# Layer statistics and a normalization moved to ScalarE in a fused feed-forward, attention, feed-forward kernel

## The chip, the cores and the metric

One Trainium2 chip, of which the kernel uses one core. The metric is the device time of one launch in microseconds. An execution varies from launch to launch, so the time is a median of three runs.

## The reference

The input `x` has 16 sequences of 256 tokens with 256 features, all in float32. Three layers follow each other, each with a residual:

```python
x = x + 0.5 * ffn(layernorm(x), w1, b1, w2, b2)
x = x + attention(layernorm(x), Wq, Wk, Wv, Wo)
x = x + 0.5 * ffn(layernorm(x), w1, b1, w2, b2)
```

`layernorm` subtracts the mean over the features and divides by `sqrt(var + 1e-5)`. `ffn` is `gelu(x @ w1q.T + b1) @ w2q.T + b2` with 1024 hidden features, and `w1q`, `w2q` are the weights rounded to three values (-1, 0, 1 after scaling by the mean of their magnitudes). `attention` has 16 heads of 16 features, rotary positions, a causal mask and a softmax over the keys.

So every token needs a mean and a variance three times: before the first feed-forward (statistics 0), before attention (statistics 1) and before the second feed-forward (statistics 2).

## The kernel before

All of `x` stays in SBUF as eight blocks of 512 tokens, `xs[0]` to `xs[7]`. A block is four tiles of 128 tokens, and a sequence is two tiles, so a block holds two sequences. All instructions of an engine run in the order in which the Python code issues them: the helper `InOrder` (line 197, which is why nearly every row of the profile says L197) pins that order. There is no planner. The order is written by hand.

The program has three stretches. The first is the feed-forward over eight blocks (`ffn(0, ...)`), in steps of one 128-feature slice of the hidden layer, eight steps a block. The second is attention, and the third is the second feed-forward. Each overlaps the next a little.

**Attention runs in turns.** The loop at line 827 runs turn `b` from 1 to 14, and each turn has eight slots `p` (line 828); `slot` (line 736) issues all the work of a slot. In turn `b` each slot takes two heads of sequence `b` through the scores with queries as rows (PSUM tiles `m`, whose row maxima VectorE takes) and two heads of sequence `b - 1` through the scores with keys as rows (PSUM tile `w`, to which VectorE adds the mask and of which ScalarE takes the exponential into `pT`). Beside that the slots carry, a piece each, the projections of sequence `b + 1`, its rotation (`rotate`), its split into a rounded part and a rest (`part`), the DMAs that place it head by head (`place`), the weighted sums of sequences `b - 1` and `b - 2` (`attend`, `turn_sums`, `divide`, `turn_out`), and the output projection of `b - 2`.

The order of a slot on each engine, as far as it matters here:

- TensorE: the score matmuls first. There are two `m` buffers, and a slot fills both, so the scores of the next slot wait until VectorE has taken the maxima out of them. Then the slot's projections and sums.
- VectorE: four maxima (`masked`, L641) with their accumulator reads, then the mask addition (`w<-w,mask_k`, L657), then what else the slot has: in slots 1 and 5 the transpose `avs`, in slots 2 and 6 `inv`, in slots 4 and 7 the transpose `oT`, and statistics.
- ScalarE: copies out of PSUM as projections finish, the exponential (L660), and in slots 1 and 5 the copy `parts<-maxes` that starts the splitting of the maxima (`part_max`, L542). Slots 3 and 6 have the rounding copy of `part`.
- GpSimd: in slot 0 the normalization of a coming sequence (`ready_x(b + 2)`, L758), then in slots 1 and 2 the three small operations of `part_max`, the rotation's `cosT`, `sinT` and the sum, and the product `o` (`divide`, L689). In slot 3 comes `split` (`part`), and in slots 4 to 6 the same chain once more for the other eight heads, ending with the second `part`.

**Where statistics come from.** `stats` (L208) is a pair on VectorE, `bn_stats` and `bn_aggr`, for a tile of 128 tokens. `finish_stats` (L213) turns the variances of several tiles into `rstd` with two small GpSimd operations, `var` and `rstd`. For attention, `after_first` (L444) puts a block's four pairs and its `finish_stats` into the list `later`; the first feed-forward takes one off each step. Ten entries, those of blocks 6 and 7, are left when the turns begin, and the turns take them off in slots 1, 3, 5 and 7 (L792): turn 1 has four pairs, turn 2 a `finish_stats` in slot 1 and pairs in 3, 5 and 7, turn 3 a pair in slot 1 and the last `finish_stats` in slot 3. For the second feed-forward, `last_stats` (L725) takes the eight tiles of the first two blocks in slot 3 of turns 6 to 13, a pair a turn, with a `finish_stats` every second turn (turns 7, 9, 11, 13).

`normalize` (L223) is one `tensor_scalar` (subtract the mean, multiply by `rstd`) on the engine that it is given; `ready_x` (L467) calls it for the two tiles of a sequence, and inside the turns that engine is GpSimd.

Of the kernel before, what the change touches and what calls it, by code (L numbers as in the profile page):

```python
# [8 lines left out]
FP = mybir.dt.float32  # L9
FR = mybir.dt.float32r  # L10
BF = mybir.dt.bfloat16
AF = mybir.ActivationFunctionType
ALU = mybir.AluOpType
# [3 lines left out]
P = 128  # L17
D = 256
# [12 lines left out]
def kernel(  # L31
# [15 lines left out]
    NB = NT // S  # L47
    NTILE = NT // P
# [5 lines left out]
    state = ctx.enter_context(tc.tile_pool(name="state", bufs=1))  # L54
    small = ctx.enter_context(tc.tile_pool(name="small", bufs=4))
# [54 lines left out]
    for at in range(0, P, HD):  # L110
        r, n = at // 32, at // HD % 2
# [53 lines left out]
    power = const.tile([P, BT], FP, name="power")  # L165
# [19 lines left out]

    mv = [state.tile([P, NTILE, 2], FP, name=f"mv_{i}") for i in range(3)]
    rstd = [state.tile([P, NTILE], FP, name=f"rstd_{i}") for i in range(3)]

    class InOrder:

# [10 lines left out]
    tensor, vector, scalar, gpsimd, sync = (  # L201
        InOrder(engine) for engine in (nc.tensor, nc.vector, nc.scalar, nc.gpsimd, nc.sync)
    )

    def tokens(n):
        return xs[n // BT][:, n % BT, :]

    def stats(ln, n):  # L208
        st = small.tile([P, 6], FP, name="st")
        vector.bn_stats(st, tokens(n))  # L210
        vector.bn_aggr(mv[ln][:, n, :], st)

    def finish_stats(ln, first, n):  # L213

        var = small.tile([P, BT], FP, name="var")
        gpsimd.tensor_scalar(
            var[:, 0:n], mv[ln][:, first : first + n, 1], LN_EPS, 1.0, ALU.add, ALU.mult
        )
        gpsimd.tensor_tensor(
            rstd[ln][:, first : first + n], var[:, 0:n], power[:, 0:n], ALU.pow  # L220
        )

    def normalize(ln, n, to, engine=None):  # L223
        (engine or vector).tensor_scalar(
            to,
            tokens(n),
            mv[ln][:, n, 0:1],
            rstd[ln][:, n : n + 1],
            ALU.subtract,
            ALU.mult,  # L230
        )
# [210 lines left out]
    later = []  # L442
# [8 lines left out]
    xn_a, xnT, qkT, o, oT, y_a = {}, {}, {}, {}, {}, {}  # L451
# [15 lines left out]
    def ready_x(b, engine=gpsimd):  # L467
        xn_a[b] = pp.tile([P, 2, D], FP, name="xn_a", bufs=1)
        for c in range(2):
            normalize(1, 2 * b + c, xn_a[b][:, c, :], engine)  # L470

    def turn_x(b):

        tp = ps_mm.tile([P, KC, S], FP, name="mm")
        for k in range(KC):
            for c in range(2):
                tensor.transpose(
                    tp[:, k, c * P : (c + 1) * P], xn_a[b][:, c, k * P : (k + 1) * P], ident
                )
        xnT[b] = pp.tile([P, KC, S], FP, name="xnT_a", bufs=3)  # L480
        scalar.copy(xnT[b], tp)
# [31 lines left out]
    def part(b, j):  # L513
        high = split[j][:, 0:2, :]
        scalar.copy(high, qk[j])
        gpsimd.tensor_sub(split[j][:, 3:1:-1, :], qk[j], high.bitcast(FP))
# [147 lines left out]
    def attend(b, half):  # L664

        av = ps_mm.tile([P, 2, S], FP, name="mm")
        for n in range(2):
            g = 2 * half + n
            for c in range(2):
                for r in range(4):  # L670
                    tensor.matmul(
                        av[32 * r : 32 * r + 32, n, c * P : S],
                        vals[b % 2][:, c, 4 * g + r, :],
                        pT[b, 2 * g + r // 2][:, r % 2, c * S : S + c * P],
                        start=(c == 0),
                        stop=(c == 1),
                    )
        sums[b, half] = av
# [40 lines left out]
    def add_out(b):  # L719
        y, tiles = y_a.pop(b)  # L720
        at = 2 * b % BT + tiles[0]
        xt = xs[2 * b // BT][:, at : at + len(tiles), :]
        vector.tensor_add(xt, y, xt)

    def last_stats(b, c):  # L725
        stats(2, 2 * b + c)
        if c == 1:
            finish_stats(2, 2 * b, 2)

# [4 lines left out]
    def slot(b, p, more=lambda: None):  # L736
        bw, bm = (n if 0 <= n < NB else None for n in (b - 1, b))
        up, now, past, last = (n if 0 <= n < NB else None for n in (b + 1, b, b - 1, b - 2))
        first = 0 if b == NB - 1 else 1
        if p == 0 and 0 <= b - 3 < NB:  # L740
            add_out(b - 3)
        if p == 6 and last is not None and b < NB - 1:
            add_out(last)
        weigh = scores(bw, p, bm, p ^ 1)
        if p == first and last is not None:
            attend(last, 1)
        if p == 5:
            if b + 2 < NB:
                turn_x(b + 2)
            if last is not None and b < NB - 1:  # L750
                project_out(last, range(1))
        for n, j, at in ((now, 0, 5), (past, 1, 1)):
            if n is not None and p == at:
                part_max(n, j)
        if p == 3 and past is not None:
            turn_max(past, 1)
        if p == 0 and b >= 1 and b + 2 < NB:
            ready_x(b + 2)  # L758
        for n, at in ((past, p + 8), (now, p)):
            slots = VALUES.get(n, (2, 6))  # L760
            if n is not None and at in slots:
                project_v(n, slots.index(at))
        if p in (0, 3) and up is not None:
            project_qk(up, p // 2, 0 if b == 0 and p == 0 else 1)
        if p == 2 and up is not None:
            project_qk(up, 1, 0, 1)
        if p in (1, 2, 4, 5) and up is not None:
            rotate(up, p // 4, *((0,) if p in (1, 4) else (1, 2)))
        if p == 4 and past is not None:
            attend(past, 0)  # L770
        if up is not None and p == 4:
            place(up, 0)
        if now is not None and p == 0:
            place(now, 1)
        if p == 6 and now is not None:
            turn_max(now, 0)
        if p == 7:
            if last is not None and b < NB - 1:
                project_out(last, range(1, 2))
            if b + 2 < NB:  # L780
                project_qk(b + 2, 0, 0, 1)
        more()
        weigh()
        if up is not None and p in (3, 6):
            part(up, p // 3 - 1)
        for n, half, at in ((last, 1, p - first), (past, 0, p - 4)):
            if n is not None and at in (0, 1, 3):
                (turn_sums, divide, None, turn_out)[at](n, half)
        if p == 3 and b - 6 in range(8):
            last_stats(*divmod(b - 6, 2))  # L790

        if b >= 1 and p % 2 == 1 and later:  # L792
            later.pop(0)()


# [29 lines left out]
    for p in range(FFN_STEPS - HEAD, 8):  # L825
        slot(0, p)
# [116 lines left out]
```

## Time and profile before

| | |
|---|---|
| median of 3 runs | 581.95 us (579.21 to 584.72) |
| the profiled execution | 581.4 us, of which the span of the profile is 579.6 us |
| TensorE | busy 560.1 us (97%) |
| VectorE | busy 473.2 us (82%) |
| GpSimd | busy 382.5 us (66%) |
| ScalarE | busy 361.8 us (62%) |
| the turns (1 to 14) | from about 164 us to 414 us of the span |

In the profile PE is TensorE, DVE VectorE, ACT ScalarE, POOL GpSimd and SP the queue that issues most DMAs. The shares of busy time are averages over three stretches with different limits: VectorE is busy 16 of every 20 us at 80 to 100 us and 19.7 of 20 us at 300 to 320 us. A row of the timeline gives the start, the duration, the engine, the operation, the tile written and the tiles read, and in brackets how long the engine had been idle and who ended that.

### The profile page before, as it was taken

How to read it: one execution, taken by the hardware profiler on the slowest of the kernel's cores; microseconds unless marked ns; L12 is line 12 of the kernel's file. 1: busy time of each engine (PE TensorE's matmuls, PEld its weight loads, DVE VectorE, ACT ScalarE, POOL GpSimd, SP SyncE). 2: the span in 40 equal slices, each digit the busy share in tenths (PEclk: the TensorE clock that was granted, in tenths of full speed). 3: DMA queues.
4: the chain of work that ended last, by engine and by line, in shares of the span. 5: the costliest groups of instructions: out<-in, count | busy, mean ns of one | idle time of the engine just before them, and what ended most of it. 6: DMA issues, size and time to landing. Idle time of an engine off the chain costs nothing.

```text
span 579.6 us, 15188 instructions
## 1 busy us (share of the span) xinstructions
PE 560.1 (97%) x5654; PEld 454.8 (78%) x5654; DVE 473.2 (82%) x1691; ACT 361.8 (62%) x637; POOL 382.5 (66%) x427
## 2 busy tenths in 40 slices
PE   3999999999999999999999999999989999999996
PEld 3788999888777677777777777777767889888886
DVE  6887778789688999999999999999986566666653
ACT  4666777675555665656666666565566666666664
POOL 4636656668478878888888988888832455445542
PEclk9999999999988999999999999999999999999999
DMA  8700000020533464544645535445500011111111
GB/s 284 236 1 2 1 1 1 28 64 26 120 93 92 112 148 98 123 106 116 147 109 123 124 94 142 121 119 129 126 6 1 1 37 36 38 37 37 37 37 36
DMA packets 35641, 46.23 MB, mean 80 GB/s; under 512 B 4464, under 2 KB 27120, under 8 KB 35568
## 3 DMA queue, kind: packets, MB, share of 16 engines
q1 hardware_dynamic: 35008, 44.35, 29.5%
q8 instruction: 44, 0.72, 0.5%
q10 hardware_dynamic: 560, 0.92, 0.4%
q14 instruction: 29, 0.24, 0.1%
HBM read 7.51 MB, written 4.19 MB: 20 GB/s over the span
## 4 chain that ended last, share of the span: by engine, by line
PE 80%; DVE 9%; issue 3%; ACT 3%; DMA 2%; POOL 2%; SPq 0%; DVEq 0%; POOLq 0%; ACTq 0%
PE mm L197 30%; PE w L197 26%; PE m L197 24%; DVE masked L197 2%; DMA qkT<-w 1%; DVE w L197 1%; DMA w<-in_w1T_dram 1%; DVE avs L197 1%; DVE maxes L197 1%; DVE w2q L197 1%; ACT h_high L197 1%; ACT h_whole L197 1%; ACT pT L197 1%; DVE st L197 1%; DVE x L197 0%
## 5 line engine op out<-in xcount | busy, mean ns | idle before, releaser
L197 DVE CUSTOM_DVE_ANT_0 masked<-m,mask_q 128x128 f32<-128x128 f32 x480 | 141.7, 351 | 11.1 <-PE w L197 7.6
L197 PE MATMUL m<-xnT,w1q 128*128 128x512 f32 x504 | 143.2, 405 | 0.7 <-ACT xnT L197 0.7
L197 ACT ACTIVATE pT<-w 128x768 f32<-128x768 f32 x128 | 104.0, 813 | 62.4 <-DVE w L197 61.1
L197 ACT ACTIVATE h_high<-m,b_sb 128x512 fp32r<-128x512 f32 x126 | 86.9, 690 | 77.5 <-PE m L197 77.3
L197 DVE TENSOR_TENSOR h_rest<-h_whole,h_high 128x512 fp32r<-128x512 f32 x86 | 82.3, 960 | 55.3 <-ACT h_whole L197 54.5
L197 PE MATMUL w<-w2q,h_high 128*128 128x256 f32 x480 | 121.4, 286 | 0.1
L197 PE MATMUL w<-w2q,h_rest 128*128 128x256 f32 x480 | 118.8, 281 | 0.3 <-POOL h_rest L197 0.3
L197 POOL TENSOR_TENSOR h_rest<-h_whole,h_high 128x512 fp32r<-128x512 f32 x42 | 55.8, 1329 | 85.7 <-ACT h_whole L197 84.5
L197 PEld LDWEIGHTS m<-xnT,w1q 128*128 128x128 f32 x504 | 87.8, 191 | 15.6 <-DVE xnT L197 2.5
L197 PE MATMUL w<-qkT 32*128 32x256 f32 (+1 forms) x1088 | 95.4, 293 | 1.3 <-DVE maxes L197 0.6
L197 PEld LDWEIGHTS w<-w2q,h_high 128*128 128x128 f32 x480 | 90.4, 188 | 4.8 <-DVE w2q L197 0.8
L197 PEld LDWEIGHTS w<-w2q,h_rest 128*128 128x128 f32 x480 | 90.3, 188 | 4.7 <-POOL h_rest L197 0.5
L197 PE MATMUL m<-qkT 32*128 32x256 f32 x960 | 90.3, 291 | 1.7 <-DVE maxes L197 0.9
L197 DVE TENSOR_TENSOR w<-w,mask_k 128x512 f32<-128x512 f32 x123 | 85.5, 695 | 2.4 <-PE w L197 2.2
L197 ACT ACTIVATE h_whole<-m,b_sb 128x512 f32<-128x512 f32 x126 | 85.9, 682 | 0.0
L197 PEld LDWEIGHTS w<-qkT 32*128 32x128 f32 x1088 | 78.0, 185 | 2.5 <-DVE maxes L197 1.1
L197 PEld LDWEIGHTS m<-qkT 32*128 32x128 f32 x960 | 69.9, 185 | 6.5 <-DVE maxes L197 4.6
L197 PE MATMUL mm<-xnT_a,wqk 128*128 128x256 f32 x256 | 69.7, 398 | 0.0
L197 PEld LDWEIGHTS mm<-xnT_a,wqk 128*128 128x128 f32 x256 | 47.0, 194 | 6.6
L197 PE MATMUL mm<-pT,vals 128*32 128x256 f32 (+1 forms) x1024 | 49.5, 329 | 0.0
L197 POOL TENSOR_TENSOR w<-w,sinT 128x512 f32<-128x512 f32 x32 | 41.4, 1293 | 5.7 <-DMA w<-w 5.7
L197 PE MATMUL w<-mT,ones 32*128 32x384 bf16 x256 | 43.2, 334 | 0.8 <-ACT mT L197 0.6
(99 smaller groups left out, 917.4 us busy)
## 6 DMA issues: line engine op xcount, KB each, us to landing
qkT<-split SPq DMA_DIRECT2D x64, 192.0 KB, 3.5
qkT<-w SPq DMA_DIRECT2D x64, 192.0 KB, 3.5
w<-w SPq DMA_DIRECT2D x64, 128.0 KB, 2.0
out_dram<-x SPq DMA_DIRECT2D x15, 256.0 KB, 2.3
x<-in_x_dram SPq DMA_DIRECT2D x7, 512.0 KB, 10.0
w<-in_w2T_dram SPq DMA_DIRECT2D x1, 1024.0 KB, 7.9
w<-in_w1T_dram SPq DMA_DIRECT2D x1, 512.0 KB, 5.5
w<-in_w1T_dram ACTq DMA_DIRECT2D x1, 512.0 KB, 5.9
```

The lines of the kernel that those rows point to most:

```text
L197: return tc.keep_in_program_order(getattr(self.engine, name)(*args, **kwargs))
```

## The change

Three things change in the turns.

1. `last_stats` no longer uses VectorE. In slot 1 ScalarE sums a tile's features (`sum_tokens`: Identity with an accumulated output) and GpSimd makes the negative mean of it (`shift`); in slot 4 ScalarE squares the tile with `shift` as bias and accumulates (`sum_squares`), and GpSimd writes mean and variance into `mv` with two more small operations, followed every second turn by `finish_stats`.
2. `ready_x` in the turns is on ScalarE: an Identity with `rstd` as scale and a new per-token `offset` as bias. It stands after the slot's exponential, no longer ahead of the slot's projections. `offset` (minus mean times `rstd`) is made in `finish_stats` for statistics 1, by two more small GpSimd operations. The normalizations ahead of the turns stay where they are.
3. `later` is taken from in slot 1 alone, so the ten entries that are left spread over turns 1 to 10: pairs in turns 1 to 4 and 6 to 9, `finish_stats` in turns 5 and 10.

```diff
+    offset = state.tile([P, NTILE], FP, name="offset")
...
-        gpsimd.tensor_tensor(
-            rstd[ln][:, first : first + n], var[:, 0:n], power[:, 0:n], ALU.pow
-        )
+        of = slice(first, first + n)
+        gpsimd.tensor_tensor(rstd[ln][:, of], var[:, 0:n], power[:, 0:n], ALU.pow)
+        if ln == 1:
+            gpsimd.tensor_tensor(offset[:, of], mv[ln][:, of, 0], rstd[ln][:, of], ALU.mult)
+            gpsimd.tensor_scalar(offset[:, of], offset[:, of], -1.0, 0.0, ALU.mult, ALU.add)
+
+    shift = {}
+
+    def sum_tokens(n):
+        total = small.tile([P, 1], FP, name="total", bufs=2)
+        scalar.activation(left_over(), tokens(n), AF.Identity, accum_out=total)
+        shift[n] = small.tile([P, 1], FP, name="shift", bufs=2)
+        gpsimd.tensor_scalar(shift[n], total, -1.0 / D, 0.0, ALU.mult, ALU.add)
+
+    def sum_squares(ln, n):
+        total = small.tile([P, 1], FP, name="squares", bufs=2)
+        scalar.activation(left_over(), tokens(n), AF.Square, bias=shift[n], accum_out=total)
+        gpsimd.tensor_scalar(mv[ln][:, n, 0:1], shift.pop(n), -1.0, 0.0, ALU.mult, ALU.add)
+        gpsimd.tensor_scalar(mv[ln][:, n, 1:2], total, 1.0 / D, 0.0, ALU.mult, ALU.add)
+
+    def left_over():
+        return small.tile([P, D], FP, name="left_over", bufs=1)
...
     def ready_x(b, engine=gpsimd):
         xn_a[b] = pp.tile([P, 2, D], FP, name="xn_a", bufs=1)
         for c in range(2):
-            normalize(1, 2 * b + c, xn_a[b][:, c, :], engine)
+            n = 2 * b + c
+            if engine is scalar:
+                scalar.activation(
+                    xn_a[b][:, c, :],
+                    tokens(n),
+                    AF.Identity,
+                    bias=offset[:, n : n + 1],
+                    scale=rstd[1][:, n : n + 1],
+                )
+            else:
+                normalize(1, n, xn_a[b][:, c, :], engine)
...
-    def last_stats(b, c):
-        stats(2, 2 * b + c)
-        if c == 1:
-            finish_stats(2, 2 * b, 2)
+    def last_stats(b, c, part):
+        if part == 0:
+            sum_tokens(2 * b + c)
+        else:
+            sum_squares(2, 2 * b + c)
+            if c == 1:
+                finish_stats(2, 2 * b, 2)
...
-        if p == 0 and b >= 1 and b + 2 < NB:
-            ready_x(b + 2)
...
         weigh()
+        if p == 0 and b >= 1 and b + 2 < NB:
+            ready_x(b + 2, scalar)
...
-        if p == 3 and b - 6 in range(8):
-            last_stats(*divmod(b - 6, 2))
-
-        if b >= 1 and p % 2 == 1 and later:
+        if p in (1, 4) and b - 6 in range(8):
+            last_stats(*divmod(b - 6, 2), p // 4)
+
+        if b >= 1 and p == 1 and later:
             later.pop(0)()
```

## The prediction

> **What bounds the kernel now.** I read the busy shares by stretch first, then turn by turn, then the timeline of single slots. In the turns TensorE and VectorE are both nearly full, so a busy share can't say which one a saving would reach. The table of three turns does. It gives a stretch, its length, and the busy time (count) of TensorE, of its weight loads, of VectorE, ScalarE and GpSimd, then clock and DMA:
>
> ```profile
> 360.70:378.55 17.85, 17.85 (x250) 13.40 (x249) 17.37 (x83) 11.38 (x22) 15.77 (x20) 1.00 0.48 119
> 378.55:396.11 17.56, 17.56 (x250) 13.20 (x249) 17.27 (x83) 10.60 (x21) 14.82 (x19) 1.00 0.49 122
> 396.11:413.99 17.88, 17.70 (x247) 13.06 (x245) 16.98 (x83) 10.78 (x21) 13.39 (x18) 1.00 0.48 120
> ```
>
> These are turns 12, 13 and 14 (from mask addition to mask addition of the last slot before). Turn 14 has no statistics at all, 0.3 us less VectorE work, and takes no less time. The VectorE timeline of slots 3 to 4 shows why, turn 13 first, then turn 14:
>
> ```profile
> 387.21 0.70 DVE L197 TENSOR_TENSOR w<-w,mask_k 128x512 f32<-128x512 f32 x1
> 387.81 0.42 DVE L197 BATCH_NORM_STATS2 st<-x 128x6 f32<-128x256 f32 x1
> 388.26 0.18 DVE L197 BATCH_NORM_AGGREGATE mv<-st 128x2 f32<-128x6 f32 x1
> ...
> 389.45 0.69 DVE L197 TENSOR_TENSOR w<-w,mask_k 128x512 f32<-128x512 f32 x1
> ```
>
> ```profile
> 405.08 0.69 DVE L197 TENSOR_TENSOR w<-w,mask_k 128x512 f32<-128x512 f32 x1
> 406.21 0.29 DVE L197 CUSTOM_DVE_ANT_0 masked<-m,mask_q 128x128 f32<-128x128 f32 x1 [0.43 <-PE w L197]
> ...
> 407.32 0.70 DVE L197 TENSOR_TENSOR w<-w,mask_k 128x512 f32<-128x512 f32 x1
> ```
>
> From one mask addition to the next it is 2.24 us with the pair and 2.24 without: where the pair stood, VectorE waits 0.43 us for the scores. TensorE sets this slot. Slot 1 is different. Turn 3 has a pair there, turn 11 has none:
>
> ```profile
> 203.81 0.70 DVE L197 TENSOR_TENSOR w<-w,mask_k 128x512 f32<-128x512 f32 x1
> ...
> 205.04 0.39 DVE L197 BATCH_NORM_STATS2 st<-x 128x6 f32<-128x256 f32 x1
> ...
> 206.64 0.69 DVE L197 TENSOR_TENSOR w<-w,mask_k 128x512 f32<-128x512 f32 x1
> ```
>
> ```profile
> 347.52 0.69 DVE L197 TENSOR_TENSOR w<-w,mask_k 128x512 f32<-128x512 f32 x1
> ...
> 349.83 0.69 DVE L197 TENSOR_TENSOR w<-w,mask_k 128x512 f32<-128x512 f32 x1
> ```
>
> 2.83 us against 2.31: VectorE sets this slot (it has the transpose `avs` too), and a pair costs its whole 0.52. Up to the mask addition of slot 4 some comes back: 6.98 us in turn 3 (to 210.79), 6.52 in turn 11 (to 354.04). So a pair in slot 1 costs about 0.44 us net, a pair in slot 3 nothing.
>
> GpSimd is the third party. Its chain from `split` in slot 3 to the product `o`, which VectorE must transpose in slot 7, is just long enough to be late when `finish_stats` is in it (turn 11):
>
> ```profile
> 354.19 1.28 POOL L197 TENSOR_TENSOR split<-w,split 128x512 fp32r<-128x512 f32 x1 [1.80 <-ACT split L197]
> 355.56 0.19 POOL L197 TENSOR_SCALAR var<-mv 128x2 f32<-128x2 f32 x1
> 355.84 0.72 POOL L197 TENSOR_TENSOR rstd<-var,power 128x2 f32<-128x2 f32 x1
> ...
> 361.03 0.62 POOL L197 TENSOR_TENSOR o<-avs,inv 128x256 f32<-128x256 f32 x1
> ```
>
> ```profile
> 361.68 0.45 DVE L197 STREAM_TRANSPOSE oT<-o 128x256 f32<-128x256 f32 x1 [0.29 <-POOL o L197]
> ```
>
> In even turns the same transpose doesn't wait. That 0.29 is the difference between turn 12 (17.85) and turn 13 (17.56).
>
> **The change, term by term.** The sum is made against the profiled execution, 581.4 us; that is 0.55 below the median of 581.95.
>
> *The last two blocks' pairs.* The changed program's order takes six pairs out of turns 1 and 2 (slots 3, 5, 7) and puts six into slot 1 of turns 2, 4, 6, 7, 8 and 9. Cost of the six: 6 x 0.44 = +2.6 us; bounds 0 (TensorE takes all the slack back) and 6 x 0.52 = 3.1. Gain: slot 3 nothing, as above; slot 5 of turn 1 about 0.4 (2.35 us, where 1.9 is what VectorE's other work takes); in turn 2 slots 5 and 7 take 2.68 and 2.90 us where the same slots without a pair take 2.14 and 2.38, so 1.06. Together -1.5. Slot 7 of turn 1 is held by the clock, below.
>
> *`finish_stats` out of slot 3 of turn 3.* In turn 4 VectorE waits 0.39 us for `o` behind it, and slots 7 and 0 take 2.08 and 2.87 us against 1.87 and 2.38; 0.13 comes back in the slot after. -0.55 us.
>
> *`finish_stats` into slot 1 of turns 5 and 10.* There it has four operations. `var` and `rstd` took 1.28 us in turn 2 (186.75 to 188.03). The two for `offset` aren't in the trace; rows nearest are the small `parts` operations of part_max, 0.23 us each, 0.32 from start to start when one waits for the other. So 2 x 0.33 = 0.65 (bounds 0.2 and 2 x 1.1, the price of `rstd`), and about 1.95 in all. Ahead of it GpSimd starts later than now: `rest` waits for ScalarE's `parts`, which now stands behind the two normalizations. An activation on 128x256 with two per-token operands isn't in the trace either: the copy of that size took 0.373 us, a 128x512 activation with a bias 0.69 against 0.587 for the copy, so 0.373 + 2 x 0.1 = 0.58, less 0.1 where one starts before the last ends (bounds 0.37 and GpSimd's 1.22). The pair delays `parts` by about 1.0 us. Normally that is free: in turn 11 `o` in slot 2 would end at 352.39 + 1.0, the ScalarE copy before `split` starts at 353.50 anyway, and VectorE takes this `o` at 354.64. With `finish_stats` it ends at 352.39 + 1.0 + 1.95 = 355.35, 0.7 us late; in turn 10 `shift` (0.2) adds to that, and the second half of the turn starts late as well. 0.7 + 1.0 = +1.7 us; bounds 0 and 4.
>
> *Statistics of the finished sequences.* Leaving slot 3 of turns 6 to 13: 0, as turn 14 shows; VectorE then waits for TensorE, and that is what is late next. On ScalarE the sum is 0.4 + 0.19 (the accumulator read's row), the squares 0.48 + 0.19. ScalarE waits 0.5 to 1.0 us ahead of most exponentials for VectorE's mask, and both stand behind an exponential; behind them wait the copies `vals` (ready just as the sum ends) and `xnT_a` (0.6 late, needed two slots on). Cost 0; without that cover each would be 0.6 x 8. On GpSimd the two `mv` operations stand between `cosT` and `rest` in the half of the turn that is late already: 2 x 0.17 us. In turns 7, 9, 11 and 13 this lengthens the wait for `o` one to one: 4 x 0.35 = +1.4 us (bounds 0 and 4 x 0.75). In the even ones there is 0.75 us of room (`o` ends at 378.41, wanted at 379.16).
>
> *The normalization off GpSimd.* 13 x 2.43 us leave an engine whose first half of a turn ends in a wait of 1.5 to 1.8 us for `split`; that wait grows, nothing else moves. 0. The exponential of slot 1 has 1.15 us free ahead of it for the pair's 1.0.
>
> *`offset` in the first feed-forward.* 0.65 us on a GpSimd that waits 1.2 us or more for VectorE or ScalarE once a block. 0.
>
> *The clock.* TensorE ran at half clock for 3.4 us in turn 1:
>
> ```profile
> 174.90:178.30 3.40, 2.87 (x41) 2.01 (x41) 3.30 (x16) 2.10 (x6) 2.85 (x6) 1.00 0.88 207
> 178.30:181.70 3.40, 3.40 (x25) 2.37 (x23) 2.38 (x11) 2.08 (x4) 3.25 (x4) 0.50 0.12 25
> ```
>
> Before it TensorE was busy 2.87 of 3.40 us, with 0.6 us of waits for VectorE's maxima, and a pair stood right there (175.54). Slot 7 took 3.67 us, the next 2.28; at full clock 2.24 and 1.95: 1.7 us. With the pair gone the window should be over 95% busy, and windows that full were never followed by half clock in this profile. I take -1.7, at a chance of six in ten. The Trainium skill ("TensorE: Matmul & The Clock Gate", "What's actually happening") says that the clock falls after at least one idle window of about 3.4 us. By that rule no window here should have been halved, since none was idle, and the term would be 0; the row above disagrees with the rule.
>
> A rule that speaks against the change is in "ScalarE: Activation LUTs", "What ACT_TABLE_LOAD costs" and "Table sets: the hidden batching unit": a function outside the loaded set costs a switch of about 2.66 us. If Square were outside the set of Exp, two switches in each of eight turns would make 43 us by that page; the changed program's order has three table loads, as before, so that term is 0.
>
> *Sum:* +2.6 - 1.5 - 0.55 + 1.7 + 1.4 - 1.7 = +2.0, so 583.4, and 584.0 set beside the median.
>
> **Rivals.** *The half clock stays* (0.25): everything as above without -1.7, so 585.7. *VectorE is the bound after all* (0.06): each of the eight pairs that leave VectorE for good is worth 0.52, and the 1.6 us that it waits for `o` in the turns goes with GpSimd's relief: 581.95 - 4.2 - 1.6 = 576.1, 1% faster. Turn 14 speaks against it. *ScalarE's pair becomes the turn's chain* (0.2), slower: the exponential of slot 1 stands behind it. It has 1.15 us free ahead, and TensorE needs its PSUM buffer about 0.9 us after it ends, so it decides from a pair of 2.0 us on. At GpSimd's price, 2.4, it costs 0.4 a turn and the GpSimd chain behind it as much again: 13 x 0.8 = 10 us less what overlaps, some 5, on top of the forecast: 589. That the change doesn't do what it says is in part so: only eight pairs leave VectorE, the other six change places.
>
> **Numbers.** Forecast case 0.49, the others as given. 1% (5.8 us) is about what a measurement of this kernel tells from no change, and both likely cases lie within. Low end: six pairs at half price, no late chains, full clock: 579. High end: half clock, chains at their upper bounds: 590. Faster by over 1% 0.06, within 1% 0.74, slower by over 1% 0.20.
>
> **What would show it.** Right: slot 3 at 2.24 us with a VectorE wait for scores in turns 6 to 13; slot 1 at 2.83 in the turns with a pair; waits for `o` of 0.6 us after turns 7, 9, 11, 13, and in turns 5 and 10 in slot 4; clock 1.00 at 178 to 182 us. Wrong: slot 3 shorter than 2.24, the exponential of slot 1 waiting for ScalarE itself, or `o` never late.

## The result, and the profile after

| | before | after |
|---|---|---|
| median | 581.4 us (578.44 to 584.72, 20 runs) | 584.05 us (582.49 to 587.35, 20 runs) |
| ratio, with its 95% interval | | 1.0057 (1.0039 to 1.0076) |
| span of the profiled execution, mean granted clock | 579.6 us, 0.992 | 582.3 us, 0.997 |
| VectorE / ScalarE / GpSimd busy | 473.2 / 361.8 / 382.5 us | 468.7 / 379.7 / 357.5 us |
| first mask addition | 162.33 us | 164.13 us |
| turns 1 to 14, from the mask addition in slot 0 | 255.91 us | 256.54 us |
| from there to the last mask addition | 25.69 us | 25.69 us |
| from the last mask addition to the end | 135.7 us | 136.0 us |

The 581.95 us that the forecast was set beside was a median of three runs; over 20 runs the kernel before has 581.4. The ratio is near that of the means (583.98 against 580.75 us); the two medians alone would give 1.0046. The time of a slot is counted from its mask addition to the next.

Two thirds of the 2.7 us between the two profiled executions had gone by before the turns began, and the turns as a whole moved by only 0.6 us. Both need taking apart, because large terms of both signs cancel in them.

First the lines that answer to those shown of before. The table of turns 12, 13 and 14 in the kernel after (a stretch, its length, the busy time and count of TensorE, weight loads, VectorE, ScalarE and GpSimd, then clock and DMA):

```profile
362.74:380.72 17.98, 17.86 (x249) 13.39 (x249) 16.98 (x83) 13.09 (x28) 13.83 (x21) 1.00 0.49 119
380.72:398.46 17.74, 17.50 (x250) 13.12 (x249) 16.87 (x83) 12.37 (x27) 12.89 (x21) 1.00 0.50 121
398.46:416.42 17.96, 17.67 (x246) 13.02 (x244) 17.12 (x83) 10.77 (x21) 13.45 (x18) 1.00 0.49 119
```

Against 17.85, 17.56 and 17.88 each turn is longer by 0.1 to 0.2 us, although VectorE has 0.4 us less to do in turns 12 and 13 and GpSimd 1.9 us less. The VectorE timeline after, slot 3 to 4 of turn 13, where the pair was taken out:

```profile
389.37 0.70 DVE L198 TENSOR_TENSOR w<-w,mask_k 128x512 f32<-128x512 f32 x1
390.50 0.29 DVE L198 CUSTOM_DVE_ANT_0 masked<-m,mask_q 128x128 f32<-128x128 f32 x1 [0.44 <-PE w L198]
...
391.62 0.69 DVE L198 TENSOR_TENSOR w<-w,mask_k 128x512 f32<-128x512 f32 x1
```

It is 2.25 us, as with the pair, and in the pair's place stands a wait of 0.44 us for scores. The same view for slot 1 of turn 4, where the change put a pair in:

```profile
221.10 0.69 DVE L198 TENSOR_TENSOR w<-w,mask_k 128x512 f32<-128x512 f32 x1
...
222.33 0.38 DVE L198 BATCH_NORM_STATS2 st<-x 128x6 f32<-128x256 f32 x1
...
223.93 0.69 DVE L198 TENSOR_TENSOR w<-w,mask_k 128x512 f32<-128x512 f32 x1
```

2.83 us, against 2.31 without. The third party, GpSimd, in the half of turn 11 that was late already:

```profile
357.31 1.27 POOL L198 TENSOR_TENSOR w<-w,cosT 128x512 f32<-128x512 f32 x1
358.55 0.18 POOL L198 TENSOR_SCALAR mv<-shift 128x1 f32<-128x1 f32 x1
358.70 0.18 POOL L198 TENSOR_SCALAR mv<-squares 128x1 f32<-128x1 f32 x1
358.96 0.19 POOL L198 TENSOR_SCALAR var<-mv 128x2 f32<-128x2 f32 x1
...
363.18 0.62 POOL L198 TENSOR_TENSOR o<-avs,inv 128x256 f32<-128x256 f32 x1
```

The two new `mv` operations take 0.41 us from start to start of the next, and the product `o` ends at 363.8. VectorE waits for it in slot 7 of turn 11, and, with `finish_stats` ahead of it, in slot 4 of turn 5, which is new:

```profile
246.92 0.45 DVE L198 STREAM_TRANSPOSE oT<-o 128x256 f32<-128x256 f32 x1 [0.59 <-POOL o L198]
...
363.83 0.45 DVE L198 STREAM_TRANSPOSE oT<-o 128x256 f32<-128x256 f32 x1 [0.40 <-POOL o L198]
```

And the two stretches of turn 1 of which the second ran at half clock before:

```profile
174.90:178.30 3.40, 3.05 (x49) 2.37 (x43) 3.32 (x19) 2.87 (x7) 3.08 (x6) 1.00 0.54 124
178.30:181.70 3.40, 3.23 (x43) 2.45 (x42) 3.28 (x16) 2.25 (x6) 3.17 (x4) 1.00 0.66 150
```

### The profile page after: what moved, and what is told of

It reads as the page before. It is cut to its first block, busy times and chain, and to the rows that moved or that the text cites. A ratio compares the mean times of both kernels' runs of the same rounds, so it can differ in the third digit from the quotient of the medians.

```text
span 582.3 us, 15256 instructions
## 1 busy us (share of the span) xinstructions
PE 559.7 (96%) x5654; PEld 455.2 (78%) x5654; DVE 468.7 (80%) x1675; ACT 379.7 (65%) x695; POOL 357.5 (61%) x441
## 4 chain that ended last, share of the span: by engine, by line
PE 73%; DVE 13%; POOL 5%; issue 5%; ACT 3%; DMA 1%; DVEq 0%; SPq 0%; POOLq 0%; ACTq 0%
PE w L198 25%; PE mm L198 24%; PE m L198 23%; DVE masked L198 3%; DVE w L198 2%; POOL w L198 2%; DVE avs L198 2%; DVE maxes L198 1%; POOL rstd L198 1%; DMA w<-in_w1T_dram 1%; DVE h_rest L198 1%; DVE w2q L198 1%; ACT h_high L198 1%; DVE st L198 1%; POOL o L198 1%
```

## The experiments

None of the kernels leaves any work out. Each was timed beside the kernel before on its chip. The granted clock of an execution matters for reading them: in the 98 executions of the kernel before that stand beside the experiments, those at a mean granted clock of 0.998 or more (40 of them) have a median of 578.9 us, and those at 0.994 (21) one of 582.2 us. The last column of this table therefore gives the median of the executions at 0.998 or more, which are called those at full clock below. The stretches are of the one profiled execution of each.

| kernel | ratio (95%) | first mask addition | turn 1 | turns 2, 3 | turns 4 to 14 | turn 15 | median at clock 0.998 or more (runs) |
|---|---|---|---|---|---|---|---|
| before | | 162.33 | 20.34 | 37.86 | 197.71 | 25.69 | 578.9 (40 of 98) |
| after | 1.0057 (1.0039 to 1.0076) | 164.13 | 18.58 | 36.40 | 201.57 | 25.69 | 582.5 (9 of 20) |
| pairs_alone | 0.9992 (0.9964 to 1.0019) | 163.00 | 16.96 | 36.46 | 198.94 | 30.36 | 578.7 (6 of 12) |
| stats_alone | 1.0012 (0.9985 to 1.0039) | 162.81 | 20.46 | 37.89 | 198.55 | 28.88 | 579.3 (4 of 12) |
| norm_alone | 1.0033 (1.001 to 1.0056) | 164.19 | 20.40 | 38.69 | 198.34 | 28.84 | 581.0 (5 of 12) |
| last_in_slot1 | 1.0053 (1.0023 to 1.0083) | 162.60 | 20.36 | 37.81 | 199.34 | 28.84 | 580.3 (3 of 12) |
| offset_vector | 1.028 (1.0252 to 1.0308) | 173.47 | 18.67 | 36.16 | 201.72 | 25.70 | none of 6 |
| offset_twice | 1.0124 (1.0098 to 1.0149) | 166.54 | 18.28 | 36.36 | 201.45 | 28.82 | 584.4 (1 of 6) |
| offset_once | 1.0056 (1.0031 to 1.0082) | 163.59 | 16.97 | 36.36 | 201.45 | 28.82 | 581.7 (3 of 12) |
| finish_slot7 | 1.0012 (0.9991 to 1.0034) | 164.30 | 16.96 | 36.35 | 198.25 | 28.83 | 579.4 (7 of 12) |
| best | 1.0176 (1.0147 to 1.0204) | 174.63 | 17.13 | 36.14 | 197.21 | 25.69 | none of 5 |
| order_alone | 0.9964 (0.994 to 0.9987) | 162.81 | 18.25 | 37.02 | 196.63 | 25.71 | 577.1 (4 of 12) |
| best_2 | 0.9937 (0.9913 to 0.9961) | 163.07 | 16.93 | 35.78 | 196.16 | 25.69 | 576.4 (8 of 12) |
| stats_order | 0.994 (0.9916 to 0.9964) | 162.67 | 16.89 | 36.14 | 197.63 | 28.80 | 575.8 (6 of 12) |

In turn 15 a value of 28.8 or more instead of 25.7 is a stretch at half clock. In turn 1 there are two, some 1.5 us each: 17.0 is without either, 18.2 to 18.7 with the one at its start, and 20.4 with both. The second stands in the four kernels with a pair in slot 7 of turn 1 and in none of the other ten. The one at the start of turn 1 comes and goes without a change in the work ahead of it: pairs_alone and stats_alone have the same first feed-forward, and only stats_alone has it. The last section shows that case.

### The three parts of the change, one at a time

Part 3 alone, `later` in slot 1 only:

```diff
-        if b >= 1 and p % 2 == 1 and later:
+        if b >= 1 and p == 1 and later:
```

> The kernel before with the third part of the change alone: the ten entries of `later` are taken in slot 1 only; statistics and normalization stay where they were. Theory of the slots (slot 3 is TensorE's, slot 1 VectorE's): six pairs leave turns 1 and 2 (-1.7 us, as the changed kernel's slots 5 and 7 showed: -0.3 - 0.3 - 0.5 - 0.5) and six enter slot 1 at 0.42 each (+2.5); the late o behind turn 3 goes (-0.6); finish_stats in slot 1 of turns 5 and 10 has two operations and a GpSimd that isn't delayed by ScalarE, so its o ends at 353.7 on the scale of turn 11, before 354.6: 0. Half clock in turn 1 gone: -1.5. Sum -1.3 us, ratio 0.998; with the half clock still there 1.000. Rival (VectorE is the bound all through the turns, a pair costs the same in any slot): no slot moves, ratio 1.000, but then slot 1 with a pair would be no longer than without; the profile tells these apart by slot 1 of turns 6 to 9 (2.83 against 2.32 us) and slot 3 (2.24 with a pair still in it).

Part 1 alone keeps the sums and squares on ScalarE (`sum_tokens`, `sum_squares`) and takes the normalization and `later` back to where they were:

> The kernel before with the first part alone: the statistics of the eight finished tiles on ScalarE, the small operations on GpSimd; normalization on GpSimd and the ten entries in slots 1, 3, 5 and 7 as before. Theory of the slots: taking the pairs out of slot 3 of turns 6 to 13 gains nothing (2.24 us with or without), the two mv operations ahead of finish_stats make the late o of turns 7, 9, 11 and 13 later by 0.3 each: +1.2 us, ratio 1.002. Rival (VectorE is the bound): 8 pairs x 0.52 = -4.2 us, ratio 0.993.

Part 2 alone keeps `ready_x(b + 2, scalar)` and `offset`, and takes the statistics and `later` back:

> The kernel before with the second part alone: the normalization in the turns on ScalarE, with the offset operations in every finish_stats for attention; statistics stay on VectorE and the ten entries in slots 1, 3, 5 and 7. Theory: GpSimd's 2.4 us a turn are worth nothing because it waits for split anyway; the offset operations delay GpSimd's bias addition in the first feed-forward, and the VectorE operations that read two SBUF operands or normalize beside it wait for it: the first mask addition comes 1.8 us later as in the changed kernel; in turn 2 the longer finish_stats makes o late by about 0.6, in turn 3 it adds 0.5 to the late o. Sum +2.5 to +3, ratio 1.005. Rival (GpSimd's relief pays): the four waits of 0.29 for o go and nothing else: -1.2 us, ratio 0.998.

By the executions at full clock (4 to 6 of each) the parts cost -0.2, +0.4 and +2.1 us, together +2.3, while the whole change costs 3.6. What pairs_alone and stats_alone don't have are the waits for `o` in slot 4 of turns 5 and 10 (0.59 and 0.91 us in the kernel after, slots longer by 0.69 and 0.86). Three things meet there: a `finish_stats` in slot 1, its `offset` operations, and a GpSimd chain that starts behind the normalization on ScalarE. In pairs_alone, with `finish_stats` in slot 1 of turns 5 and 10 and nothing of part 2, VectorE doesn't wait for `o`. norm_alone has all three in turn 2, and the wait too:

```profile
194.66 0.45 DVE L198 STREAM_TRANSPOSE oT<-o 128x256 f32<-128x256 f32 x1 [0.62 <-POOL o L198]
```

Its slot 4 of turn 2 takes 3.36 us, against 2.64 before. The whole change has two such turns where norm_alone has one, which is some 0.8 us of the 1.3 that the whole costs more than its parts. Which half of part 2 makes the wait, the `offset` operations or the later start, no run separates.

No part gains beyond the noise. In pairs_alone slot 1 of turns 6 to 9 takes 2.83 us and slot 3, with a pair still in it, 2.28, so slots do move, against its rival. In stats_alone slot 3 of turn 11 takes 2.24 us with a wait of 0.44 for scores; relieving VectorE there is worth nothing. That rival of the theory (0.993 for part 1) is refuted, and so is 0.998 for part 2.

### The cost of a slot for the same pair

The kernel before with its eight pairs of finished sequences in slot 1:

```diff
-        if p == 3 and b - 6 in range(8):
+        if p == 1 and b - 6 in range(8):
```

> The kernel before with one thing moved: the eight pairs of the finished tiles stand in slot 1 of turns 6 to 13 instead of slot 3, with their finish_stats. Same work on every engine. Theory of the slots: each pair costs 0.42 in slot 1 and frees nothing in slot 3: +3.4 us; finish_stats moves out of the late half of the turn, so the four waits of 0.29 for o go: -1.2. Sum +2.2, ratio 1.004; slot 1 at 2.83 us in those turns, slot 3 at 2.24 with a VectorE wait of 0.4 for the scores. Rival (VectorE is the bound, a pair costs the same anywhere): only the o waits go, -1.2, ratio 0.998.

Slot 1 of turns 6 to 13 goes from 2.32 to 2.83 us. Slot 3 takes 2.27 or 2.28 us without its pair, 2.24 to 2.27 with it, except in three slots (turns 6 and 10 before, turn 7 here) where TensorE waits for a transfer, which is told below. The time is 1.0053 (1.0023 to 1.0083) of before. The same work on the same engine costs half a microsecond a turn in one slot and nothing in the other.

### `offset` in the first feed-forward

The later start of the turns, 1.8 us, seemed to be the term that I had set to 0. Three kernels were made for it. In offset_vector VectorE does the two operations in the first feed-forward, in offset_twice GpSimd does them twice, and in offset_once GpSimd does them once for all 18 tiles in turn 1:

```diff
-            gpsimd.tensor_tensor(offset[:, of], mv[ln][:, of, 0], rstd[ln][:, of], ALU.mult)
-            gpsimd.tensor_scalar(offset[:, of], offset[:, of], -1.0, 0.0, ALU.mult, ALU.add)
+            by = vector if first < (NBLK - 2) * BT else gpsimd
+            by.tensor_tensor(offset[:, of], mv[ln][:, of, 0], rstd[ln][:, of], ALU.mult)
+            by.tensor_scalar(offset[:, of], offset[:, of], -1.0, 0.0, ALU.mult, ALU.add)
```

> The changed kernel, with the two operations for offset of blocks 0 to 5 (the ones made in the first feed-forward) on VectorE in place of GpSimd; everything else as changed. Theory: the 1.8 us by which the changed kernel reaches the first mask addition later (164.13 against 162.33) come from these two operations: on GpSimd they delay the rotation's bias addition behind them, and VectorE operations beside that wait for it. On VectorE, which has idle time there, they cost about nothing: first mask addition back at 162 to 163, time 1.8 us under the changed kernel's, 1.0025 of the kernel before. Rival: the delay is from elsewhere (another start of the first feed-forward, DMAs): first mask addition stays at 164 and the time at 1.0057. Second rival: VectorE is as full there as GpSimd, and the operations cost 0.4 x 6 = 2.4 us there too: 1.006.

> The changed kernel, with the same two GpSimd operations for offset in blocks 0 to 5 made twice. Theory (as for the run with them on VectorE): the first mask addition moves by about as much again, 1 to 2 us later than the changed kernel's 164.13, and the time to 1.007 to 1.009 of the kernel before. Rival (the delay was one lost race for a port or a DMA, not the time of these operations): 164 and 1.0057 as the changed kernel.

```diff
-        if ln == 1:
+        if ln == 1 and first >= (NBLK - 2) * BT:
...
+        if (b, p) == (1, 0):
+            offsets(slice(6, (NBLK - 2) * BT))
```

> The changed kernel, with offset of tiles 6 to 23 (blocks 0 to 5) made by two GpSimd operations on 18 columns in slot 0 of turn 1, in place of twelve on 4 columns in the first feed-forward. GpSimd has no normalization there any more. Theory (the twelve operations delay the bias addition and the rotation on GpSimd, and nothing else brings the 1.8 us): first mask addition back near 162.3, turns as in the changed kernel, time 1.0026 of the kernel before. Rival (the first feed-forward is late for another reason): 164 and 1.0057.

offset_vector was some 16 us slower than the kernel before (1.028), where I expected it to be faster than the changed one. The timeline shows both engines at the end of a block's statistics:

```profile
63.31 1.01 POOL L198 TENSOR_TENSOR rstd<-var,power 128x4 f32<-128x4 f32 x1
...
64.28 2.39 POOL L198 TENSOR_TENSOR x<-x,b_sb 128x1024 f32<-128x1024 f32 x1
64.35 2.35 DVE L198 TENSOR_TENSOR offset<-mv,rstd 128x4 f32<-128x4 f32 x1 [1.03 <-POOL rstd L198]
...
66.73 0.17 DVE L198 TENSOR_SCALAR offset<-offset 128x4 f32<-128x4 f32 x1
```

VectorE first waits 1.03 us for GpSimd's `rstd`, and then an operation on four columns takes 2.35 us and ends at 66.70, when GpSimd's bias addition ends (66.67). All that VectorE has queued behind it stands still, and each of the first four blocks moves the feed-forward by 1.9 us (steps 16, 24, 32 and 40 start 2.4, 4.3, 6.2 and 8.2 us later than before). Moving work off a slow engine put the slow engine into the queue of the fast one.

The same effect measures what the two operations cost on GpSimd. Two engines in one view, around the normalization of sequence 1 by VectorE; first before, then offset_once, after, and offset_twice:

```profile
93.62 2.57 POOL L197 TENSOR_TENSOR x<-x,b_sb 128x1024 f32<-128x1024 f32 x1
...
95.00 1.66 DVE L197 TENSOR_SCALAR xn_a<-x,mv,rstd 128x256 f32<-128x256 f32 x2
```

```profile
94.19 2.61 POOL L198 TENSOR_TENSOR x<-x,b_sb 128x1024 f32<-128x1024 f32 x1
...
95.61 1.67 DVE L198 TENSOR_SCALAR xn_a<-x,mv,rstd 128x256 f32<-128x256 f32 x2
```

```profile
94.25 0.29 POOL L198 TENSOR_TENSOR offset<-mv,rstd 128x4 f32<-128x4 f32 x1
...
94.63 0.19 POOL L198 TENSOR_SCALAR offset<-offset 128x4 f32<-128x4 f32 x1
...
94.78 2.40 POOL L198 TENSOR_TENSOR x<-x,b_sb 128x1024 f32<-128x1024 f32 x1
...
95.55 1.78 DVE L198 TENSOR_SCALAR xn_a<-x,mv,rstd 128x256 f32<-128x256 f32 x1
```

```profile
96.39 2.40 POOL L198 TENSOR_TENSOR x<-x,b_sb 128x1024 f32<-128x1024 f32 x1
...
96.60 2.34 DVE L198 TENSOR_SCALAR xn_a<-x,mv,rstd 128x256 f32<-128x256 f32 x1
```

A normalization of this size takes VectorE 0.40 us alone. Beside the bias addition it ends when that ends: at 97.33 against 97.18 after, at 98.94 against 98.79 in offset_twice. So what delays GpSimd by 0.6 us delays VectorE's next step here by 0.43 (the pair takes 2.10 us after and 1.67 in offset_once), and twice the operations delay it further. The Trainium skill ("SBUF — State Buffer", "SBUF: two separate sides") says that some VectorE instructions (with two inputs in SBUF, or in a mode that uses two ports) and those of GpSimd need the same pair of ports, and that one instruction holds it to its end while the other is fully blocked. These rows agree with it.

But the theory of the 1.8 us fell in part. offset_once, with no `offset` in the first feed-forward, still reaches the first mask addition at 163.59, and its time is 1.0056, the rival's number, where I expected 1.0026. Against the changed kernel it gains 0.54 us there, and 0.8 between the medians at full clock (3 and 9 executions). Doubling costs 2.4 there, more than the 1 to 2 us expected, and the time is 1.0124 where I expected 1.007 to 1.009. The other 1.26 us has three parts. 0.2 is there from the first steps on; the profile of before is the earliest of all there, the others are 0.1 to 0.5 later. About 0.5 is a jump at step 51, where GpSimd's `rstd` took 1.03 us in before and 1.46 in pairs_alone. With the first feed-forward of the kernel before, pairs_alone and stats_alone have this jump, and last_in_slot1 and order_alone don't, so the change isn't what makes it. The last 0.4 us builds up between steps 8 and 40 in after, offset_once, best_2 and finish_slot7; what makes it is open.

### GpSimd's small operations in slot 7

The changed kernel with `mv` and `finish_stats` of the finished sequences, and both `finish_stats` for attention, issued in slot 7:

```diff
-        if p in (1, 4) and b - 6 in range(8):
-            last_stats(*divmod(b - 6, 2), p // 4)
+        if p in (1, 4, 7) and b - 6 in range(8):
+            last_stats(*divmod(b - 6, 2), p // 3)
...
-        if b >= 1 and p == 1 and later:
+        if b >= 1 and later and p == (7 if len(later) in (1, 6) else 1):
```

> The changed kernel, with GpSimd's small statistics operations moved to slot 7 of their turns: the two mv operations with finish_stats of the finished sequences from slot 4, and the two finish_stats for attention from slot 1 of turns 5 and 10. In slot 7 GpSimd waits about 3 us for ScalarE's copy of the maxima; pairs stay in slot 1. Theory: the late products o are what the change costs in turns 5 and 10 (0.7 and 0.9 us) and in turns 7, 9, 11 and 13 (0.27 each more, on 0.29 each from before), so 1.6 + 4 x 0.56 = 3.8 us at most, 2.3 at least since part of each wait comes back a slot later: 0.9995 to 1.002 of the kernel before, and no wait of VectorE for o in slot 4 of turn 5 and 10 or in slot 7 of the odd turns. Rival: the wait for o stands beside a wait of TensorE's that is as long, and the time stays at 1.0057.

1.0012 (0.9991 to 1.0034), as the theory had it. Turns 4 to 14 shrink from 201.57 to 198.25 us, 3.3 less, and VectorE waits for `o` in none of them. GpSimd in turn 11, as shown above for the kernel after:

```profile
358.23 0.62 POOL L198 TENSOR_TENSOR o<-avs,inv 128x256 f32<-128x256 f32 x1
359.18 1.28 POOL L198 TENSOR_TENSOR w<-w 128x512 fp32r<-128x512 f32 x1 [0.33 <-ACT w L198]
360.43 0.19 POOL L198 TENSOR_SCALAR mv<-shift 128x1 f32<-128x1 f32 x1
...
361.12 0.71 POOL L198 TENSOR_TENSOR rstd<-var,power 128x2 f32<-128x2 f32 x1
```

The same four operations, now behind `o` and the second `part`, where GpSimd would only wait. At full clock the kernel is 3.1 us faster than the kernel after (579.4 against 582.5). Some 1.2 of these (4 x 0.29) are waits in turns 7, 9, 11 and 13 that the kernel before has too, so the late `o` made some 1.9 of the 3.6 us that the change costs at full clock.

### Versions that beat both kernels

best: offset_vector, finish_slot7 and the pairs left for attention one a turn in slot 3 of turns 1 to 8. best_2: the same with `offset` made once in turn 1.

> The changed kernel with what the runs so far point to: offset of blocks 0 to 5 on VectorE, GpSimd's small statistics operations in slot 7 (as in the run with these alone), and the pairs for attention that are left one a turn in slot 3 of turns 1 to 8, where VectorE otherwise waits for scores, not in slot 1. Theory, against the kernel before: pairs out of turns 1 and 2 -1.5, finish_stats out of turn 3 -0.55, no half clock in turn 1 -1.5, no late o in the odd turns -1.2, pairs in slot 3 0: -4.7, that is 0.992. Rival (TensorE sets the turns whatever waits go, and what VectorE gains is lost to TensorE's own waits): 0.997 to 1.0.

> The changed kernel with offset made once in turn 1, GpSimd's small statistics operations in slot 7, and the pairs left for attention one a turn in slot 3 of turns 1 to 8. Theory: the run with the same order of the turns took 5.4 us off from first to last mask addition (276.16 against 281.60), and made it good by offset on VectorE; without that the first mask addition is at 162.3 and the time 5.4 under the kernel before: 0.991. Rival (offset in turn 1 holds GpSimd or the first normalization, or the turns' gain hung on their later start): 0.996 to 1.0.

best is at 1.0176 where I expected 0.992. It reaches its first mask addition at 174.63, for the reason shown for offset_vector; its turns 1 to 14 take 250.47 us, against 255.91. best_2 has no such price: 0.9937 (0.9913 to 0.9961), a smaller gain than the 0.991 that I expected.

Is any of that due to ScalarE? order_alone moves no work to ScalarE; it only changes places in the kernel before:

```diff
+    ready = []
...
-            finish_stats(2, 2 * b, 2)
+            ready.append(lambda: finish_stats(2, 2 * b, 2))
...
-        if b >= 1 and p % 2 == 1 and later:
-            later.pop(0)()
+        if p == 2 and b >= 1 and len(later) in (1, 6):
+            later.pop(0)()
+        if p == 2 and ready:
+            ready.pop()()
+        if later and len(later) not in (1, 6) and p in ((), (3,), (1, 3), (1, 3), (1, 3), (3,))[min(b, 5)]:
+            later.pop(0)()
```

> The kernel before, with no work moved to ScalarE at all: only the places of its own operations are changed. The pairs left for attention go into slot 3 of turns 1 to 5 and slot 1 of turns 2, 3 and 4 (none in slots 5 and 7); every finish_stats in the turns is issued in slot 2 behind the product o, where GpSimd waits 1.5 to 1.8 us for the split copy, those of the finished sequences a turn later. Theory (the places make the time, the engine doesn't): slot 1 of turn 1 -0.36, its slot 5 -0.3, its half clock -1.5, turn 2 -1.06, turn 3 -0.55, the late o in four odd turns -1.6, two pairs more in slot 1 +0.8: -4.5, that is 0.992. Rival (VectorE has to be relieved of work for the turns to get shorter): 0.998 to 1.0.

stats_order takes part 1 of the change to it, so that slot 3 is free for the other pairs, and leaves the normalization on GpSimd:

> The kernel before with the first part of the change (sums and squares of the finished sequences on ScalarE), the pairs left for attention one a turn in slot 3, and GpSimd's small statistics operations in slot 2 behind the product o, a turn later. The normalizations stay on GpSimd, and there is no offset. It stands between the run that changed places alone (0.9964) and the best one (0.9937). Theory A: what the best one has over the run with places alone is the slot 3 that the finished sequences left for the other pairs (two pairs in slot 1 less, 0.8 us, and no odd turn late); the normalization on ScalarE is worth nothing: turns 4 to 14 at 196.2 us, time 0.9937 to 0.995. Theory B: GpSimd, with the normalization, can't take the small operations in slot 2 without being late with split: VectorE waits for o again, turns 4 to 14 at 197.5 us or more, 0.997 to 1.0.

Places alone give 0.9964 (0.994 to 0.9987), between the theory's 0.992 and the rival's 0.998, which the interval still holds. The turns decide: with all of VectorE's work left to it, turns 2 to 14 take 233.65 us in the profile, against 235.57, and VectorE no longer waits for `o` in turns 7 to 13. So VectorE need not be relieved of work for the turns to get shorter. With part 1 it is 0.994, near best_2, so the normalization on ScalarE is worth nothing that these runs can tell, and part 1 is worth some 1.3 us (577.1 against 575.8 at full clock, 4 and 6 executions), with intervals that overlap. On stats_order the two theories split: the time is A's, but turns 4 to 14 took 197.63 us in the profile, which is B's number. B's mechanism shows only once (a wait of 0.33 us for `o` in turn 5). What filled the turns is another wait. TensorE in slot 3 of turn 3 of stats_order:

```profile
204.08 0.33 PE L197 MATMUL w<-mT,ones 32*128 32x384 bf16 x2
204.86 0.39 PE L197 MATMUL m<-qkT 32*128 32x256 f32 x2 [0.45 <-DMA qkT<-w]
```

The scores of slot 3 wait for the DMA that places the keys and queries (`place`). That slot took 3.00 us. Over 2.40 us it takes in 3 to 6 of the turns 3 to 13 of the seven kernels whose slot 1 mostly has no pair (before 3, stats_alone 3, norm_alone 4, best 6, best_2 4, order_alone 3, stats_order 6), and in 0 to 2 of the seven that have one there in most turns (after and offset_vector 0, finish_slot7 2, the others 1). In all 35 of these slots a transfer into `qkT` lands 0.10 us before TensorE loads the weights for the scores, also where the row puts the wait down to VectorE; 33 of the 35 are in turns whose slot 1 takes 2.32 us, without a pair. A turn that gets shorter meets the landing of this transfer next. That a longer slot 1 is what gives it the time is my reading of these counts; no run changed the transfer by itself.

What these slots take above 2.25 us each adds up to 3.0 us in stats_order, 1.4 in best_2 and 1.1 in order_alone, and 1.2 in the kernel before. So it is not what kept best_2 and order_alone behind their forecasts. These had the half clock of one profile in them: 1.5 us in the sum for order_alone, and in the 5.4 us taken for best_2 most of the 3.2 us between turn 1 of before, with two stretches at half clock (20.34), and of best, with none in turn 1 (17.13). At full clock order_alone is 1.8 and best_2 2.5 us faster than before.

## Why the prediction was right, by its steps

The forecast was 584.0 us, and it is 584.05. The sum behind it (+2.0) came out at +2.7 between the profiles, and not every step held. As a change the forecast is further off than as a time: +2.0 on 581.95 is a ratio of 1.0035, just under the measured interval (1.0039 to 1.0076).

| term | forecast | profile |
|---|---|---|
| six pairs into slot 1 | +2.6 | 6 x (0.52 - 0.10) = +2.5 |
| pairs out of turns 1 and 2 | -1.5 | slots 5, 5 and 7: -0.31 - 0.54 - 0.52 = -1.4 |
| `finish_stats` out of turn 3 | -0.55 | slots 6 and 7 of turn 3 and 0 of turn 4: -0.21 - 0.50 + 0.12 = -0.58 |
| `finish_stats` in turns 5 and 10 | +1.7 | slots 0.69 + 0.86 = +1.55 |
| last pairs out of slot 3 | 0 | 0 (2.24 to 2.28 us in turns 6 to 13) |
| `mv` in turns 7, 9, 11 and 13 | +1.4 | 4 x 0.27 = +1.1 |
| normalization off GpSimd | 0 | 0 in the turns |
| the half clock at 178 us | -1.7 | slot 7 of turn 1: 3.66 to 2.20 = -1.5 |
| `offset` in the first feed-forward | 0 | +0.5, by offset_once |
| start of the turns, otherwise | not in the sum | +1.3 |
| slot 3 of turns 2, 5, 6 and 10 | not in the sum | -0.34 - 0.30 - 0.47 - 0.38 = -1.5 |

- **The turns were right.** The five terms from slots 1, 3 and the late `o` are within 0.3 us each. That a pair costs its time in slot 1 and nothing in slot 3 decided it. A pair in slot 1 was to cost 0.44 us net (the prediction's own rows, 6.98 and 6.52, give 0.46) and came out at 0.42. last_in_slot1 and best_2 show it from both sides: in best_2 the pair stands in slot 3 of turn 5, and that slot takes 2.24 us.
- **A wait's full length.** The `mv` term was to lengthen the wait for `o` to 0.6 us in the odd turns. It is 0.40; the other 0.17 us stands one slot earlier, and 0.27 in all was lost instead of 0.35.
- **The half clock was not a gain of the median.** The stretch is gone in the profile after, and in all nine other kernels without a pair in slot 7 of turn 1, while the four with it have it. The reason given for that does not hold: the stretch ahead was to be over 95% busy without the pair, and it is 90% in the row after (3.05 of 3.40 us), and just ahead of the place of the half clock, as the last section shows, no busier than before. Nor is it a sure price of the pair: of the kernel before's 98 executions 40 ran at a mean clock of 0.998 or more, where there is no room for a stretch that takes 0.003 off the mean. The mean granted clock is 0.9961 in those 98, and 0.9961 again in the 109 executions of the kernels without the pair. The step took a saving from one execution, one at 0.992, and carried it to a median, to which it belongs only by the share of executions that have it. Without that term the sum is +3.65, and at full clock the two kernels differ by 3.6 us (582.5 against 578.9), at 0.994 by 3.5 (585.7 against 582.2). That is the size of the rival in which the half clock stays (585.7, that is +3.75), to which the prediction gave 0.25; as a change it fits the measured interval, and the forecast case does not.
- **`offset` at nothing was wrong**, with 0.5 to 0.8 us. The waits of 1.2 us that I counted as cover were GpSimd's own; ahead of the bias addition it has none, and VectorE waits for that addition.
- **Luck.** The table adds up to +2.0 of the 2.7 us between the profiles; of the rest 0.3 stands behind the last mask addition, and the other 0.4 is spread over slots that moved by 0.1 to 0.2. Its two lines that were in no sum, +1.3 and -1.5, cancel. The base, 581.95, stands 0.55 us above the median of 20 runs, and the half clock took 1.7 off it: without either, the sum gives 585.05. The mechanism of the forecast in the turns is shown; that the median came within 0.1 us is not its merit.

Of the rivals, VectorE as the bound is refuted by stats_alone and by the waits for scores in slot 3. ScalarE's pair did not become the chain, but it was close: the two normalizations take 1.09 us, and ScalarE's idle time ahead of the exponential of slot 1 (read as 1.15 us, in fact 0.94 to 1.04 in turns 3 to 13 before) is down to 0.00 to 0.07. The exponential still starts 0.03 us after the mask addition ends. Part 2 alone costs 2.1 us at full clock; by the profiles its first mask addition is 1.86 us later, and slot 4 of turn 2 is 0.72 longer.

## What to carry to other kernels

Where two engines are both nearly full, ask slot by slot which wait ends last: the same operation cost 0.5 us in one slot and nothing in another, and changing places alone made the kernel faster (0.9964) where moving work to an idle engine in the wrong places made it slower (1.0057). A small operation on a slow engine costs what it delays behind it, so issue it right behind the product that others wait for. And a saving that is read from one execution's clock belongs in the sum only by the share of executions that have it.

## What the runs showed of the hardware that I had not expected

The clock. The stretches at half clock ahead of the last mask addition last 3.41 us, or two or three times that (6.83, 10.24), and in a profile with several they start a whole number of 3.41 us apart: in the kernel before at 161.20 and 178.27, five apart. So one can lay such a grid over a profile and ask how busy TensorE was in the stretch just ahead. The columns are those of the table of turns; the clock is the third from the end. At the start of turn 1, first in stats_alone and then in pairs_alone, whose work up to there is the same (its grid is that of its half clock at 427.05):

```profile
158.02:161.43 3.41, 2.76 (x40) 2.01 (x38) 3.17 (x17) 0.60 (x3) 3.14 (x5) 1.00 0.29 65
161.43:164.84 3.41, 3.41 (x24) 2.28 (x18) 2.07 (x11) 0.71 (x2) 2.78 (x3) 0.50 0.03 7
```

```profile
157.41:160.82 3.41, 2.76 (x28) 2.25 (x27) 3.02 (x17) 1.25 (x4) 2.42 (x5) 1.00 0.51 133
160.82:164.23 3.41, 3.41 (x45) 2.52 (x44) 3.09 (x20) 1.44 (x3) 2.68 (x3) 1.00 0.03 7
```

And around the end of turn 1, in the kernel before, with a pair in slot 7, and after, without it (its grid is that of its half clock at 163.08, five stretches ahead):

```profile
174.86:178.27 3.41, 2.88 (x41) 1.98 (x41) 3.31 (x17) 2.11 (x6) 2.86 (x6) 1.00 0.87 205
178.27:181.68 3.41, 3.41 (x25) 2.38 (x23) 2.39 (x11) 2.11 (x4) 3.26 (x4) 0.50 0.13 27
```

```profile
176.73:180.15 3.42, 2.90 (x43) 2.26 (x43) 3.28 (x16) 2.42 (x6) 3.02 (x6) 1.00 0.94 208
180.15:183.56 3.41, 3.41 (x46) 2.54 (x44) 3.21 (x15) 2.03 (x5) 2.19 (x3) 1.00 0.12 23
```

In each of the two cases TensorE was as busy in the stretch ahead, to 0.02 us; once the clock was halved, and once it stayed. In offset_vector a stretch of its grid with only 1.85 of 3.42 us busy (from 100.89) was followed by full clock. So the busy share of the stretch before, which the prediction went by, does not decide it alone. What does is not shown.

The second is the one seen in offset_vector: a VectorE operation on 4 columns took 2.35 us beside a GpSimd addition, and 0.17 us for the next one after it.
